# Two graph layers on one core: distances in row groups, messages by Strassen's product between the gate products

## The chip, the cores and the metric

The kernel runs on one core of a Trainium2 chip. A core has five engines that work side by side, each through its own queue in order: TensorE (PE in the profile) multiplies matrices, loading a stationary operand (PEld) and streaming a moving one past it into a memory of eight banks called PSUM; VectorE (DVE) and ScalarE (ACT) work elementwise and read PSUM; GpSimd (POOL) works elementwise on the main on-chip memory, SBUF, alone; SyncE (SP) issues transfers. The metric is the device time of one execution in microseconds. Before the change it was 2087.46 us, the median of three runs (2084.68 to 2087.62).

## What is computed

Two layers over 128 graphs of 128 nodes with 256 features, all in float32. The change lies in the second layer, which in the reference, cut to what matters, is this:

```python
xc = jnp.transpose(x, (0, 2, 1))
h = jax.nn.relu(_bn(_conv1d(xc, conv1_w, 0), bn1_g, bn1_b, bn1_m, bn1_v))
h = _bn(_conv1d(h, conv2_w, 8), bn2_g, bn2_b, bn2_m, bn2_v)
x_conv = jnp.transpose(jax.nn.relu(h + xc), (0, 2, 1))
s = x @ w_se.T + b_se                                   # 3 coordinates a node
sq = jnp.sum(s * s, axis=-1)
dist = sq[:, :, None] + sq[:, None, :] - 2.0 * jnp.einsum('bnd,bmd->bnm', s, s)
A = jnp.exp(-dist) * mask                               # mask: the adjacency
msg = jax.nn.relu(x @ w_msg.T + b_msg)
x_nmp = jnp.einsum('bnm,bmd->bnd', A, msg)
x_in = jnp.concatenate([x_conv, x_nmp], axis=-1)
gi = x_in @ w_ih.T + b_ih
gh = x @ w_hh.T + b_hh
# r, z: sigmoids of the first two thirds of gi + gh
nn_ = jnp.tanh(gi_n + r * gh_n)
return (1.0 - z) * nn_ + z * x                          # then x + this, layer norm
```

## The kernel before

There are three phases. The first (to about 740 us) runs layer 0 and the first convolution over pairs of graphs; it also makes the Fourier coefficients of the convolution's taps, with short products of 17 rows that lie in four row groups of TensorE's array (L408). The second (to about 930 us) multiplies in the Fourier domain (L503 to L530). The change is in the last phase, from 930 us to the end.

The last phase works on 32 groups of four graphs. For each group, PE runs these pieces:

- **gather** (`l1_gather`, L748): the product of messages and kernel matrix, 8 products in two banks, 16 passes in all. Every float32 product shows as two passes. ACT copies each bank to `nmpT`, and DVE makes the four sums `sm` from it.
- **messages** (`l1_project`, L693): 8 products of 128x128 by 128x256 into two banks; DVE adds the bias (L707), ACT applies the relu (L711). The function also starts the sums `sh` of x1T on POOL.
- **distances** (`l1_own`, L715, and `l1_kernel`, L735): each graph has 5 numbers a node, kept in 8 rows, in `left` and `right`. Sixteen graphs are turned together into 128 rows (`turned`). For each group, POOL multiplies `turned` by a mask for each graph into `own` (128x512), and one product of 128 rows by 512 columns gives the distances of four graphs in one bank. ACT takes the exponential (L743), DVE multiplies by the adjacency (L744) into `AT`.
- **gate** (`l1_gru`, L775), twice, each time for two graphs of a group in the two rows of a 2x2 block form: Strassen's product (Winograd's form) makes the gates with seven products instead of eight. Each of the seven has three parts (x1T, convolution, messages: `h`, `c`, `m`) of 384 columns in one bank, so six passes. DVE takes the banks in the order 0, 1, 5, 6, 4, 3, 2 (L797 to L805), POOL makes two sums beside it (L802, L803). Then comes a tail: tanh on ACT (L808), DVE L815 and L816, tanh (L817), DVE L819 to L822, and the layer norm (L247, L248, L152, L153, L255, L257).
- **synthesis** (`l1_synth`, L662), once for two groups: 16 products against a cosine table and 16 of 8 rows in four row groups, into four banks of the pool `acc`; DVE (L686) and ACT (L689) finish them, POOL makes the sums `sc`.

PSUM is split in two: `acc` has four banks for the synthesis, and `psC` has four which gather, messages, distances and gate take in turn. A piece that wants a bank waits until the one that used it four turns ago has been read.

PE's order is written out by hand, that of the other engines is a planner's: it simulates the program and gives each engine, whenever it is free, the ready operation that comes first in the program. The loop of the last phase (L843) is for each group g: start the loads of group g + 2; gather g; `own` and messages of g + 1; gate of the first half of g; distances of g + 1; in odd iterations the synthesis of the next two groups; gate of the second half of g. Ahead of the loop, a prologue makes own, messages, and distances of groups 0 and 1, the weight sums (`l1_factors`, L617) and the first synthesis.

Of the kernel before, what the change touches and what calls it, by code (L numbers as in the profile page):

```python
# [20 lines left out]
CO = 3  # L21
KD = 8
GD = P // KD
PAD = TAPS // 2
L = P + PAD
M = L
# [7 lines left out]
def gnn_layers_kernel(ctx: ExitStack, tc: tile.TileContext, a: dict, out: bass.AP):  # L34
# [332 lines left out]
    def l1_front(p):  # L367
        s = st[p]
        h = s["h"] = wk.tile([P, J, D], F32, tag="h", name=f"h_{p}")
        for j in range(J):  # L370
            ph = bank(f"conv1_ps_{p}_{j}")
            for c in range(NC):
                nc.tensor.matmul(  # L373
                    ph[:, 0 : D + CO], lhsT=s["x1T"][:, c, nodes(j)], rhs=conv1_w[:, c, :],
                    start=(c == 0), stop=(c == NC - 1),
                )
            nc.vector.tensor_tensor(h[:, j, :], ph[:, 0:D], shift1, ALU.add)
            nc.scalar.activation(coords[:, p * J + j, :], ph[:, D : D + CO], AF.Copy)
        nc.scalar.activation(h, h, AF.Relu)

    def l1_store(p):
# [173 lines left out]
    nc.vector.tensor_add(left[:, :, CO + 1], left[:, :, CO + 1], coords[:, :, 2])  # L555
    nc.vector.tensor_copy(right[:, :, CO], left[:, :, CO + 1])

    mask_i = cw.tile([P, GD], I32, tag="mask_i", name="mask_i")
    nc.gpsimd.iota(mask_i, pattern=[[-KD, GD]], base=0, channel_multiplier=1)
    mask_f = cw.tile([P, GD], F32, tag="mask_f", name="mask_f")  # L560
    nc.vector.tensor_copy(mask_f, mask_i)
    mask = cw.tile([P, GD], F32, tag="mask", name="mask")
    nc.vector.tensor_scalar(mask, mask_f, 0.0, None, ALU.is_ge)
    nc.vector.scalar_tensor_tensor(mask, mask_f, float(KD - 1), mask, ALU.is_le, ALU.mult)
    w_msg = weights("w_msgT", D)
    b_msg = rows("L1_gnn_b_msg", 0, D, cw)


# [36 lines left out]
    ci = cpool("ci", 3)  # L605
    cy = cpool("cy", 4)
    ck = cpool("ck", 2)
    acc = cpool("acc", 4, space=PSUM)
    psc = cpool("psC", 4, space=PSUM)

    def bankc(name):
        return psc.tile([P, 512], F32, tag="ps", name=name)

    cs = cpool("cs", 1)
    factors = {}

    def l1_factors():  # L617

        for kind, w in (("h", w_hh), ("c", w_ih[:, 0:NC]), ("m", w_ih[:, NC : 2 * NC])):
            t = cs.tile([P, 4, 3 * P], F32, tag=f"t{kind}", name=f"t_{kind}")  # L620
            b11, b12, b21, b22 = (w[:, c, h, :] for c in range(NC) for h in range(2))
            nc.vector.tensor_sub(t[:, 0, :], b12, b11)
            nc.vector.tensor_sub(t[:, 1, :], b22, t[:, 0, :])
            nc.vector.tensor_sub(t[:, 2, :], b22, b12)
            nc.vector.tensor_sub(t[:, 3, :], t[:, 1, :], b21)
            factors[kind] = (b11, b21, b22, t[:, 3, :], t[:, 0, :], t[:, 1, :], t[:, 2, :])

    def load_c(g):
        s = st[g] = {}
# [30 lines left out]


    def l1_synth(d):  # L662
        pcs = {}
        for e in range(2):
            s = st[2 * d + e]
            for c in range(NC):
                pc = pcs[e, c] = acc.tile([P, 512], F32, tag="acc", name=f"conv2_ps_{2 * d + e}_{c}")
                for q in range(G):
                    nc.tensor.matmul(  # L669
                        pc[:, nodes(q)], lhsT=sy[2 * d + e][0][:, q, c * P : (c + 1) * P], rhs=S,  # L670
                        start=(q == 0), stop=False, skip_group_check=True,
                    )
        for q in range(G):
            for e in range(2):
                for c in range(NC):
                    k = slice(32 * (NC * e + c), 32 * (NC * e + c) + ML)
                    nc.tensor.matmul(
                        pcs[e, c][:, nodes(q)], lhsT=sy[2 * d + e][1][k, q, :], rhs=SL[k, :],
                        start=False, stop=(q == G - 1), skip_group_check=True,
                    )  # L680
        for e in range(2):
            s = st[2 * d + e]
            s["xcT"] = ck.tile([P, NC, G * P], F32, tag="xcT", bufs=3, name=f"xcT_{2 * d + e}")
            for c in range(NC):
                dst = s["xcT"][:, c, :]
                nc.vector.scalar_tensor_tensor(  # L686
                    dst, pcs[e, c], scale2[:, c : c + 1], s["x1T"][:, c, :], ALU.mult, ALU.add
                )
                nc.scalar.activation(dst, dst, AF.Relu, bias=shift2[:, c : c + 1])  # L689
            l1_sums(2 * d + e, "c", s["xcT"], nc.gpsimd)  # L690


    def l1_project(g):  # L693
        s = st[g]
        x1T = s["x1T"]
        l1_sums(g, "h", x1T, nc.gpsimd)
        msg = ck.tile([P, G, D], F32, tag="msg", name=f"msg_{g}")
        for pr in range(G // 2):
            pm = bankc(f"msg_ps_{g}_{pr}")
            for j in range(2):  # L700
                q = 2 * pr + j
                for c in range(NC):
                    nc.tensor.matmul(  # L703
                        pm[:, j * D : (j + 1) * D], lhsT=x1T[:, c, nodes(q)], rhs=w_msg[:, c, :],
                        start=(c == 0), stop=(c == NC - 1),
                    )
            nc.vector.tensor_tensor(  # L707
                msg[:, 2 * pr : 2 * pr + 2, :], pm.rearrange("p (j e) -> p j e", j=2),
                b_msg.unsqueeze(1).to_broadcast([P, 2, D]), ALU.add,
            )  # L710
        nc.scalar.activation(msg, msg, AF.Relu)  # L711
        s["msg"] = msg


    def l1_own(g):  # L715
        if g % (GD // G) == 0:
            pt = bankc(f"turn_ps_{g}")
            for i, v in enumerate((left, right)):
                nc.tensor.transpose(
                    pt[:, nodes(i)], v[:, g * G : g * G + GD, :].rearrange("p q k -> p (q k)"), ident  # L720
                )
            turned = ck.tile([P, 2, P], F32, tag="turned", name=f"turned_{g}")
            nc.scalar.activation(turned.rearrange("p i n -> p (i n)"), pt[:, 0 : 2 * P], AF.Copy)
            st["turned"] = turned
        turned = st["turned"]

        own = ck.tile([P, G, P], F32, tag="own", name=f"own_{g}")
        lo = g * G % GD
        nc.gpsimd.tensor_tensor(
            own, turned[:, 1, :].unsqueeze(1).to_broadcast([P, G, P]),  # L730
            mask[:, lo : lo + G].unsqueeze(2).to_broadcast([P, G, P]), ALU.mult,
        )
        st[g].update(turned=turned, own=own)

    def l1_kernel(g):  # L735
        s = st[g]
        turned, own = s["turned"], s["own"]
        pd = bankc(f"dist_ps_{g}")
        nc.tensor.matmul(  # L739
            pd, lhsT=turned[:, 0, :], rhs=own.rearrange("p q n -> p (q n)"), start=True, stop=True  # L740
        )
        AT = ck.tile([P, G * P], F32, tag="AT", name=f"AT_{g}")
        nc.scalar.activation(AT, pd, AF.Exp, scale=-1.0)  # L743
        nc.vector.tensor_mul(AT, AT, s["adjT"].rearrange("p q n -> p (q n)"))  # L744
        s["AT"] = AT

# [15 lines left out]
    def l1_sums(g, kind, src, engine):  # L762

        v = src.rearrange("p c (r j n) -> p c r j n", r=G // 2, j=2)
        a11, a12, a21, a22 = (v[:, c, :, j, :] for j in range(2) for c in range(NC))
        t = ck.tile([P, 4, G // 2, P], F32, tag=f"s{kind}", name=f"s{kind}_{g}")
        s1, s2, s3, s4 = (t[:, i] for i in range(4))
        engine.tensor_tensor(s1, a21, a22, ALU.add)
        engine.tensor_tensor(s2, s1, a11, ALU.subtract)
        engine.tensor_tensor(s3, a11, a21, ALU.subtract)  # L770
        engine.tensor_tensor(s4, a12, s2, ALU.subtract)
        st[g][f"f{kind}"] = (a11, a12, s4, a22, s1, s2, s3)


    def l1_gru(g, pr):  # L775
        s = st[g]
        x1 = s["x1"]
        y = ck.tile([P, 2, D], F32, tag="y", name=f"y_{g}_{pr}")
        add, sub = ALU.add, ALU.subtract

        def product(i):
            pg = bankc(f"g_ps_{g}_{pr}_{i}")
            for k, (kind, lo) in enumerate((("h", 0), ("c", P), ("m", P))):
                nc.tensor.matmul(  # L784
# [45 lines left out]
    with tc.manual_schedule(engines={mybir.EngineType.PE}):  # L830
# [4 lines left out]
            load_x1(g)  # L835
            l1_own(g)
        for g in range(2):
            l1_project(g)
        for g in range(2):
            l1_kernel(g)  # L840
        l1_factors()
# [1 line left out]
        for g in range(NG):  # L843
            d = g // 2
            if g + 2 < NG:
                load_c(g + 2)
                if g % 2 == 0:
                    load_y(d + 1)
                load_x1(g + 2)
            l1_gather(g)  # L850
            if 2 <= g + 1 < NG:
                l1_own(g + 1)
                l1_project(g + 1)
            l1_gru(g, 0)
            if 2 <= g + 1 < NG:
                l1_kernel(g + 1)
            if g % 2 == 1 and d + 1 < ND:
                l1_synth(d + 1)
            l1_gru(g, 1)
# [42 lines left out]
```

## Time and profile before

| | us |
|---|---|
| median of three runs | 2087.46 |
| the profiled execution | 2086.79 |
| its span in the profile | 2085.0 |
| an even iteration of the last phase | 33.2 |
| an odd one, with a synthesis | 38.1 (every other one 38.3, with two transposes) |
| in an even one, DVE busy | 23.3 |
| TensorE on the chain of the whole span: gate products | 42% |
| messages | 5% |
| gather | 3% |
| distances | 1% |

The profile is one execution, recorded by the hardware. A line of a timeline has the start in us from the span's start, the length, the engine, the line of the kernel, the operation, the tiles written and read, and in brackets, where there are any, the idle time before it and what ended it. A line of the chain has start, length, engine and tile. The chain follows the work that ended last back to what released it: what isn't on it was hidden behind something else. PE's passes overlap at their ends (a pass of 384 columns shows as 0.486 us, though the next starts 0.322 us after it), so lengths of PE's work are taken from start to start. The granted clock of TensorE was 0.994 of full speed over the span.

### The profile page before, as it was taken

What the parts mean: (1) busy time and instruction counts of PE and PEld (TensorE: products, weight loads), DVE (VectorE), ACT (ScalarE), POOL (GpSimd) and SP (SyncE); (2) the same over time, 40 slices, a digit from 0 to 9 for tenths busy, and PEclk for the clock granted to TensorE, in tenths of its full rate; (3) what the DMA queues carried; (4) which work ended last, traced back from release to release, by engine and by line L of the source; (5) the groups of instructions that cost most, each with busy time, mean ns of one, the idle gap of its engine ahead of it and who ended that gap; (6) DMA issues with size and microseconds to landing.
All of it is one profiled execution on the core that took longest, in us unless ns stands there. A gap on an engine that the chain in (4) does not pass through costs nothing.

```text
span 2085.0 us, 27437 instructions
## 1 busy us (share of the span) xinstructions
PE 2043.7 (98%) x9025; PEld 1401.6 (67%) x9025; DVE 1433.0 (69%) x2856; ACT 744.0 (36%) x1484; POOL 672.9 (32%) x889
## 2 busy tenths in 40 slices
PE   8999999999999979999999999999999999999997
PEld 5666666766667658886666666666666666666664
DVE  7777777776777744447776766676767767766766
ACT  3555555555555511112222222222222222222221
POOL 1111111111111135553343444343434434443432
PEclk9999999999999999999999999999999999999999
DMA  3444444344444469993222122212212221221100
GB/s 117 137 145 138 137 147 144 133 144 137 140 145 133 153 228 318 305 302 119 62 82 68 54 74 72 69 60 72 78 51 75 70 73 56 67 72 56 36 25 21
DMA packets 191789, 235.39 MB, mean 113 GB/s; under 512 B 16400, under 2 KB 136736, under 8 KB 191648
## 3 DMA queue, kind: packets, MB, share of 16 engines
q1 hardware_dynamic: 186160, 229.44, 33.5%
q10 hardware_dynamic: 5488, 4.21, 0.7%
q8 instruction: 72, 1.18, 0.2%
q14 instruction: 69, 0.57, 0.1%
HBM read 129.77 MB, written 103.81 MB: 112 GB/s over the span
## 4 chain that ended last, share of the span: by engine, by line
PE 95%; DVE 2%; DMA 2%; ACT 1%; issue 1%; POOL 0%; POOLq 0%; ACTq 0%; DVEq 0%; SPq 0%
PE g_ps L784 42%; PE f_ps L303 10%; PE msg_ps L703 5%; PE gate_ps L308 5%; PE conv_ps L373 5%; PE y_ps L510 5%; PE mix_ps L329 3%; PE coef_ps L391 3%; PE nmp_ps L754 3%; PE conv_ps L669 3%; PE z_ps L523 2%; PE w_ps L408 2%; PE x1T_ps L270 2%; PE wl_ps L411 1%; PE xT_ps L270 1%; PE dist_ps L739 1%
## 5 line engine op out<-in xcount | busy, mean ns | idle before, releaser
L303 PE MATMUL f_ps<-w,xT 128*128 128x512 f32 x512 | 244.1, 600 | 0.1
L808 ACT ACTIVATE o<-o 128x1024 f32<-128x1024 f32 x64 | 67.6, 1057 | 335.6 <-DVE o L805 335.6
L152 POOL TENSOR_SCALAR rstd_b<-mv_b 128x2 f32<-128x2 f32 x64 | 12.2, 191 | 501.6 <-DVE mv_b L248 501.6
L152 POOL TENSOR_SCALAR rstd_a<-mv_a 128x2 f32<-128x2 f32 x64 | 12.2, 191 | 463.9 <-DVE mv_a L248 447.9
L784 PE MATMUL g_ps<-t_c,sc 128*128 128x384 f32 x384 | 155.2, 486 | 0.0
L784 PE MATMUL g_ps<-t_m,sm 128*128 128x384 f32 x384 | 155.2, 486 | 0.0
L784 PE MATMUL g_ps<-t_h,sh 128*128 128x384 f32 x384 | 155.2, 486 | 0.0
L257 ACT ACTIVATE y<-y,nb_b,rstd_b 128x256 f32<-128x256 f32 x128 | 69.9, 593 | 218.6 <-DVE nb_b L255 218.6
L308 PEld LDWEIGHTS gate_ps<-w,xT 128*128 128x128 f32 x512 | 98.2, 192 | 69.2 <-issue 61.8
L510 PE MATMUL y_ps<-wb,H 128*128 128x256 f32 x544 | 128.9, 380 | 4.7 <-DMA wb<-w_d 2.1
L308 PE MATMUL gate_ps<-w,xT 128*128 128x256 f32 x512 | 132.2, 381 | 0.0
L802 POOL TENSOR_TENSOR u<-u,p 128x512 f32<-128x512 f32 x64 | 81.1, 1267 | 155.4 <-DVE p L801 155.4
L303 PEld LDWEIGHTS f_ps<-w,xT 128*128 128x128 f32 x512 | 88.6, 192 | 62.6 <-issue 62.2
L312 ACT ACTIVATE hom<-f_ps,norm 128x256 f32<-128x256 f32 x128 | 60.5, 473 | 187.0 <-PE f_ps L303 187.0
L518 POOL TENSOR_TENSOR ws<-wb 128x512 f32<-128x512 f32 x67 | 94.8, 1416 | 88.7 <-PE z_ps L523 60.3
L373 PE MATMUL conv_ps<-conv_w,x1T 128*128 128x259 f32 x512 | 122.6, 381 | 0.0
L510 PEld LDWEIGHTS y_ps<-wb,H 128*128 128x128 f32 x544 | 102.8, 190 | 20.5 <-issue 5.1
L703 PE MATMUL msg_ps<-w_msgT_w,cx1T 128*128 128x256 f32 x512 | 115.6, 379 | 0.0
L784 PEld LDWEIGHTS g_ps<-t_m,sm 128*128 128x128 f32 x384 | 73.0, 190 | 50.9
L784 PEld LDWEIGHTS g_ps<-t_c,sc 128*128 128x128 f32 x384 | 73.0, 190 | 50.9
L784 PEld LDWEIGHTS g_ps<-t_h,sh 128*128 128x128 f32 x384 | 72.9, 190 | 50.9 <-issue 1.2
L373 PEld LDWEIGHTS conv_ps<-conv_w,x1T 128*128 128x128 f32 x512 | 97.2, 190 | 14.4
(219 smaller groups left out, 4622.4 us busy)
## 6 DMA issues: line engine op xcount, KB each, us to landing
wb<-w_d SPq DMA_DIRECT2D x68, 512.0 KB
w_d<-w_o SPq DMA_DIRECT2D x256, 128.0 KB
y_d<-yb SPq DMA_DIRECT2D x68, 256.0 KB
x<-in_x SPq DMA_DIRECT2D x64, 256.0 KB
x_d<-x SPq DMA_DIRECT2D x64, 256.0 KB
x1T_d<-x1T SPq DMA_DIRECT2D x64, 256.0 KB
cx1T<-x1T_d SPq DMA_DIRECT2D x64, 256.0 KB
yt<-y_d SPq DMA_DIRECT2D x32, 512.0 KB
```

What stands on the lines that cost most here:

```text
L257: nc.scalar.activation(dst[:, q, :], src[:, q, :], AF.Identity, bias=nb[:, q : q + 1], scale=rstd[:, q : q + 1],)
L270: nc.tensor.transpose(t[:, (c * J + j) * P : (c * J + j + 1) * P], src[:, j, c * P : (c + 1) * P], ident,)
L303: nc.tensor.matmul(pf, lhsT=xT[:, c, nodes(j)], rhs=w0[:, c, 0 : 2 * D], start=(c == 0), stop=(c == NC - 1),)
L308: nc.tensor.matmul(pg[:, j * D : (j + 1) * D], lhsT=xT[:, c, nodes(j)], rhs=w0[:, c, 2 * D : 3 * D], start=(c == 0), stop=(c == NC - 1),)
L329: nc.tensor.matmul(pm[:, j * D : (j + 1) * D], lhsT=adjT_[:, j, :], rhs=hom[:, j, :], start=True, stop=True,)
L373: nc.tensor.matmul(ph[:, 0 : D + CO], lhsT=s["x1T"][:, c, nodes(j)], rhs=conv1_w[:, c, :], start=(c == 0), stop=(c == NC - 1),)
L510: nc.tensor.matmul(py[:, blk, :], lhsT=coefs(blk if k == 0 else 2 * k + 1 - blk, c), rhs=w[:, c, blk, :], start=(c == 0), stop=(c == NC - 1),)
L518: nc.gpsimd.tensor_tensor(ws, w[:, :, 0, :], w[:, :, 1, :], ALU.add)
L703: nc.tensor.matmul(pm[:, j * D : (j + 1) * D], lhsT=x1T[:, c, nodes(q)], rhs=w_msg[:, c, :], start=(c == 0), stop=(c == NC - 1),)
L784: nc.tensor.matmul(pg[:, lo : lo + 3 * P], lhsT=s[f"f{kind}"][i][:, pr, :], rhs=factors[kind][i], start=(k == 0), stop=(k == 2), skip_grou ...
L802: nc.gpsimd.tensor_tensor(u4, u2, p5, add)
L808: nc.scalar.activation(rz, rz, AF.Tanh, scale=0.5)
```

## The change

In the distances, the coordinates are stored in another order, so that in `turned` the graphs with the same place q in their groups share 32 rows. `own` becomes one 128x128 product with a mask of one column a group, and the distances of a group are four products of 32 rows by 128 columns, each in its own row group and its own bank. The four banks are one tile of the pool `acc`, which now has one tile of four banks that distances and synthesis take in turn. They are computed ahead of the first gate half instead of behind it, and `own` and the sums `sh` are made one group earlier, with three buffers for `sh` and one for `sm`.

The messages of groups 2 to 31 use Strassen's product as the gate does: seven products of two 128x128 halves. They come in four portions (products 0 and 1; 5 and 6; 4 and 3; 2), one bank each, issued in the first gate half ahead of its third, fourth, fifth and sixth product. DVE adds the portions up in seven operations of 128x256, POOL in two. Groups 0 and 1 keep the old form under the name `l1_project_first`.

```diff
-            nc.scalar.activation(coords[:, p * J + j, :], ph[:, D : D + CO], AF.Copy)
+            b = p * J + j
+            slot = b // GD * GD + b % G * GR + b % GD // G
+            nc.scalar.activation(coords[:, slot, :], ph[:, D : D + CO], AF.Copy)
...
+    def right_factors(pool, name, b11, b12, b21, b22):
+
+        t = pool.tile([P, 4, b11.shape[-1]], F32, tag=f"t{name}", name=f"t_{name}")
+        nc.vector.tensor_sub(t[:, 0, :], b12, b11)
+        nc.vector.tensor_sub(t[:, 1, :], b22, t[:, 0, :])
+        nc.vector.tensor_sub(t[:, 2, :], b22, b12)
+        nc.vector.tensor_sub(t[:, 3, :], t[:, 1, :], b21)
+        return b11, b21, b22, t[:, 3, :], t[:, 0, :], t[:, 1, :], t[:, 2, :]
...
-    acc = cpool("acc", 4, space=PSUM)
+    acc = cpool("acc", 1, space=PSUM)
     psc = cpool("psC", 4, space=PSUM)
...
+    nc.vector.tensor_sub(b_rest, b_msg[:, P:D], b_msg[:, 0:P])
...
     def l1_synth(d):
+        four = acc.tile([P, 4, 512], F32, tag="acc", name=f"conv2_ps_{d}")
...
     def l1_project(g):
...
+        def products(*which):
+            pm = bankc(f"msg_ps_{g}_{which[0]}")
+            for k, i in enumerate(which):
+                for r in range(2):
+                    nc.tensor.matmul(
+                        pm[:, (2 * k + r) * P : (2 * k + r + 1) * P],
+                        lhsT=s["fh"][i][:, r, :], rhs=m_factors[i], start=True, stop=True,
+                    )
...
+        pa, pb = products(0, 1)
+        v.tensor_tensor(u1, pa, bias_m[0], add)
+        v.tensor_tensor(o[:, :, 0, 0, :], pb, u1, add)
+        yield
+        pa, pb = products(5, 6)
+        v.tensor_tensor(u2, pa, u1, add)
+        v.tensor_tensor(u3, pb, u2, add)
+        yield
+        pa, pb = products(4, 3)
+        v.tensor_tensor(p5, pa, bias_m[1], add)
+        v.tensor_tensor(o[:, :, 1, 0, :], u3, pb, sub)
+        nc.gpsimd.tensor_tensor(u4, u2, p5, add)
+        nc.gpsimd.tensor_tensor(o[:, :, 1, 1, :], u3, p5, add)
+        yield
+        (pa,) = products(2)
+        v.tensor_tensor(o[:, :, 0, 1, :], pa, u4, add)
+        nc.scalar.activation(msg, msg, AF.Relu)
+        yield
...
     def l1_own(g):
...
-        own = ck.tile([P, G, P], F32, tag="own", name=f"own_{g}")
-        lo = g * G % GD
-        nc.gpsimd.tensor_tensor(
-            own, turned[:, 1, :].unsqueeze(1).to_broadcast([P, G, P]),
-            mask[:, lo : lo + G].unsqueeze(2).to_broadcast([P, G, P]), ALU.mult,
+        own = ck.tile([P, P], F32, tag="own", name=f"own_{g}")
+        nc.gpsimd.tensor_scalar(
+            own, turned[:, 1, :], mask[:, g % GR : g % GR + 1], None, ALU.mult
         )
...
     def l1_kernel(g):
...
-        pd = bankc(f"dist_ps_{g}")
-        nc.tensor.matmul(
-            pd, lhsT=turned[:, 0, :], rhs=own.rearrange("p q n -> p (q n)"), start=True, stop=True
-        )
+        pd = acc.tile([P, G, 512], F32, tag="acc", name=f"dist_ps_{g}")
+        for q in range(G):
+            k = slice(q * P // G, (q + 1) * P // G)
+            nc.tensor.matmul(
+                pd[:, q, 0:P], lhsT=turned[k, 0, :], rhs=own[k, :], start=True, stop=True
+            )
...
     def l1_sums(g, kind, src, engine):
-        t = ck.tile([P, 4, G // 2, P], F32, tag=f"s{kind}", name=f"s{kind}_{g}")
+        t = ck.tile([P, 4, G // 2, P], F32, tag=f"s{kind}", bufs={"h": 3, "c": 2, "m": 1}[kind], name=f"s{kind}_{g}")
...
-    def l1_gru(g, pr):
+    def l1_gru(g, pr, between=()):
...
         def product(i):
+            if next(made) > 1:
+                next(between, None)
...
                 load_x1(g + 2)
+                l1_own(g + 2)
+                l1_sums(g + 2, "h", st[g + 2]["x1T"], nc.gpsimd)
             l1_gather(g)
             if 2 <= g + 1 < NG:
-                l1_own(g + 1)
-                l1_project(g + 1)
-            l1_gru(g, 0)
-            if 2 <= g + 1 < NG:
                 l1_kernel(g + 1)
+            l1_gru(g, 0, l1_project(g + 1) if 2 <= g + 1 < NG else ())
             if g % 2 == 1 and d + 1 < ND:
                 l1_synth(d + 1)
             l1_gru(g, 1)
```

More of the change, by code (lines that the diff above doesn't have):

```diff
@@ L23 @@
 GD = P // KD
+GR = GD // G
 PAD = TAPS // 2
@@ L556, in gnn_layers_kernel @@
     nc.vector.tensor_copy(right[:, :, CO], left[:, :, CO + 1])
[L558 to L564, printed above, removed]
-    w_msg = weights("w_msgT", D)
+    row_i = cw.tile([P, G, GR], I32, tag="row_i", name="row_i")
+    nc.gpsimd.iota(row_i, pattern=[[-GR * KD, G], [-KD, GR]], base=0, channel_multiplier=1)
+    row_f = cw.tile([P, G, GR], F32, tag="row_f", name="row_f")
+    nc.vector.tensor_copy(row_f, row_i)
+    hit = cw.tile([P, G, GR], F32, tag="hit", name="hit")
+    nc.vector.tensor_scalar(hit, row_f, 0.0, None, ALU.is_ge)
+    nc.vector.scalar_tensor_tensor(hit, row_f, float(KD - 1), hit, ALU.is_le, ALU.mult)
+    mask = cw.tile([P, GR], F32, tag="mask", name="mask")
+    nc.vector.tensor_add(mask, hit[:, 0, :], hit[:, 1, :])
+    for q in range(2, G):
+        nc.vector.tensor_add(mask, mask, hit[:, q, :])
+    w_msg = weights("w_msgT", D)
+    def right_factors(pool, name, b11, b12, b21, b22):
[5 more added lines that the diff above has]
+        return b11, b21, b22, t[:, 3, :], t[:, 0, :], t[:, 1, :], t[:, 2, :]
+    m_factors = right_factors(
+        cw, "msg", *(w_msg[:, c, h * P : (h + 1) * P] for c in range(NC) for h in range(2))
+    )
     b_msg = rows("L1_gnn_b_msg", 0, D, cw)
@@ L614, in gnn_layers_kernel @@
     cs = cpool("cs", 1)
+    b_rest = ones
+    nc.vector.tensor_sub(b_rest, b_msg[:, P:D], b_msg[:, 0:P])
     factors = {}
@@ L619, in l1_factors @@
         for kind, w in (("h", w_hh), ("c", w_ih[:, 0:NC]), ("m", w_ih[:, NC : 2 * NC])):
[L620 to L626, printed above, removed]
+            factors[kind] = right_factors(cs, kind, *(w[:, c, h, :] for c in range(NC) for h in range(2)))
     def load_c(g):
@@ L666, in l1_synth @@
             for c in range(NC):
-                pc = pcs[e, c] = acc.tile([P, 512], F32, tag="acc", name=f"conv2_ps_{2 * d + e}_{c}")
+                pc = pcs[e, c] = four[:, NC * e + c, :]
                 for q in range(G):
@@ L694, in l1_project, with sums, l1_project_first @@
         s = st[g]
-        x1T = s["x1T"]
-        l1_sums(g, "h", x1T, nc.gpsimd)
-        msg = ck.tile([P, G, D], F32, tag="msg", name=f"msg_{g}")
+        msg = s["msg"] = ck.tile([P, G, D], F32, tag="msg", name=f"msg_{g}")
+        o = msg.rearrange("p (r j) (h n) -> p r j h n", r=2, h=2)
+        v, add, sub = nc.vector, ALU.add, ALU.subtract
+        def products(*which):
[6 more added lines that the diff above has]
+                    )
+            return [pm[:, 2 * k * P : 2 * (k + 1) * P].rearrange("p (r n) -> p r n", r=2) for k in range(len(which))]
+        def sums(name):
+            return ck.tile([P, 2, P], F32, tag=f"m{name}", bufs=1, name=f"m{name}_{g}")
+        u1, u2, u3, u4, p5 = (sums(q) for q in ("u1", "u2", "u3", "u4", "p5"))
+        bias_m = [q.unsqueeze(1).to_broadcast([P, 2, P]) for q in (b_msg[:, 0:P], b_rest)]
+        pa, pb = products(0, 1)
[16 more added lines that the diff above has]
+        yield
+    def l1_project_first(g):
+        s = st[g]
+        msg = s["msg"] = ck.tile([P, G, D], F32, tag="msg", name=f"msg_{g}")
         for pr in range(G // 2):
@@ L700, in l1_project @@
             for j in range(2):
-                q = 2 * pr + j
                 for c in range(NC):
                     nc.tensor.matmul(
-                        pm[:, j * D : (j + 1) * D], lhsT=x1T[:, c, nodes(q)], rhs=w_msg[:, c, :],
-                        start=(c == 0), stop=(c == NC - 1),
+                        pm[:, j * D : (j + 1) * D], lhsT=s["x1T"][:, c, nodes(2 * pr + j)],
+                        rhs=w_msg[:, c, :], start=(c == 0), stop=(c == NC - 1),
                     )
@@ L711, in l1_project @@
         nc.scalar.activation(msg, msg, AF.Relu)
-        s["msg"] = msg
     def l1_own(g):
@@ L737, in l1_kernel @@
         turned, own = s["turned"], s["own"]
-        pd = bankc(f"dist_ps_{g}")
-        nc.tensor.matmul(
-            pd, lhsT=turned[:, 0, :], rhs=own.rearrange("p q n -> p (q n)"), start=True, stop=True
-        )
-        AT = ck.tile([P, G * P], F32, tag="AT", name=f"AT_{g}")
-        nc.scalar.activation(AT, pd, AF.Exp, scale=-1.0)
+        pd = acc.tile([P, G, 512], F32, tag="acc", name=f"dist_ps_{g}")
[3 more added lines that the diff above has]
+                pd[:, q, 0:P], lhsT=turned[k, 0, :], rhs=own[k, :], start=True, stop=True
+            )
+        AT = ck.tile([P, G * P], F32, tag="AT", name=f"AT_{g}")
+        nc.scalar.activation(
+            AT.rearrange("p (q n) -> p q n", q=G), pd[:, :, 0:P], AF.Exp, scale=-1.0
+        )
         nc.vector.tensor_mul(AT, AT, s["adjT"].rearrange("p q n -> p (q n)"))
@@ L772, in l1_sums @@
         st[g][f"f{kind}"] = (a11, a12, s4, a22, s1, s2, s3)
-    def l1_gru(g, pr):
+    def l1_gru(g, pr, between=()):
         s = st[g]
+        between = iter(between)
         x1 = s["x1"]
@@ L779, in l1_gru @@
         add, sub = ALU.add, ALU.subtract
+        made = iter(range(7))
         def product(i):
+            if next(made) > 1:
+                next(between, None)
             pg = bankc(f"g_ps_{g}_{pr}_{i}")
@@ L837, in gnn_layers_kernel @@
         for g in range(2):
-            l1_project(g)
+            l1_sums(g, "h", st[g]["x1T"], nc.gpsimd)
+            l1_project_first(g)
         for g in range(2):
```

## The prediction

> **What bounds the kernel now.** I read the page's busy times and its chain of waits first, then the chain in order of time inside the last phase, then the timelines of VectorE (DVE) and GpSimd (POOL) beside it.
>
> ```profile
> PE 2043.7 (98%) x9025; PEld 1401.6 (67%) x9025; DVE 1433.0 (69%) x2856; ACT 744.0 (36%) x1484; POOL 672.9 (32%) x889
> PE 95%; DVE 2%; DMA 2%; ACT 1%; issue 1%; POOL 0%; POOLq 0%; ACTq 0%; DVEq 0%; SPq 0%
> ```
>
> TensorE is the end-to-end bound. In the last phase nothing else is on the chain, and each piece starts where the last one stopped:
>
> ```profile
> 1543.34 1.78 PE nmp_ps L754 x16
> 1545.12 3.46 PE msg_ps L703 x16
> 1548.58 13.54 PE g_ps L784 x42
> 1562.13 0.86 PE dist_ps L739 x2
> 1562.98 3.57 PE conv_ps L669 x32
> 1566.56 1.10 PE conv_ps L677 x32
> 1567.66 13.74 PE g_ps L784 x42
> ```
>
> So a microsecond of TensorE work removed here is gained, unless a wait takes its place. An iteration of the group loop takes 33.2 us (even) or 38.1 us (odd, with the synthesis). DVE is busy 23.3 us of 33.2 and 25.8 of 38.0 there. It isn't the bound on average, but it works in bursts. One gate product is 6 passes in 1.93 us (13.54/7).
>
> **Part 1, messages.** Removed: 16 passes of 256 columns, 3.46 us. Added: 7 products x 2 halves x 2 passes = 28 passes of 128 columns. The nearest row is nmp_ps: 16 such passes in 1.78, 0.111 each, so 3.12 us; by L669 (3.57/32) it is the same, and with that line's entry of 0.1 counted once for each of four portions it would be 3.5. I take 3.12: **-0.34** an iteration (bounds -0.34 to +0.06). Groups 0 and 1 keep the old form, so 30 iterations (1 to 30): -10.2 us.
>
> **Part 2, distances.** Removed: 0.86. Added: 4 products x 2 passes, 32 rows by 128 columns, in four row groups and four banks. The tap products of the first phase have just that shape with 512 columns:
>
> ```profile
> 312.43 1.07 PE w_ps L408 x8
> 313.50 0.98 PE wl_ps L411 x2
> 314.47 0.59 PE x1T_ps L270 x4
> 315.06 1.72 PE f_ps L303 x4
> ```
>
> A 512-column pass is 0.43 (1.72/4), so eight in a row would be 3.44, and they took 1.07: two passes deep (0.86) and 0.21 on top. For 128 columns that gives 2 x 0.111 + 0.21 = 0.43, and about 0.1 on the way back to full products (wl_ps takes 0.98 for two passes of 0.43; the first gate products behind L677 also lose 0.1). By L677, 1.10/32 x 8 = 0.28 and 0.2 for both switches, 0.48. I take 0.50: **-0.36**, 30 times -10.8, and -0.7 for the two in the prologue. Bounds: 0.28, and 1.09 if nothing overlapped (8 x 0.111 + 0.2).
>
> The Trainium skill (TensorEngine Tiling (Array Packing), Key Properties and Theoretical Speedup) promises up to 4x for 32 rows, but says that a change of tiling mode drains the array. By the 4x alone the distances would cost 0.22 and the 30 iterations would gain 19; the rows above show 3.2x and 0.2 to 0.3 us of switching, and the rows are used.
>
> **Part 3, work that moves to DVE and POOL.** DVE's two message adds (0.68) become seven of 128x256 out of PSUM. The first phase has that shape (h<-conv_ps at L377: 0.42), so +1.6 us an iteration, DVE from 70 to 75%. POOL gets two 128x256 adds (0.73, as L768) and its `own` shrinks from 1.04-1.16 to something between 0.19 (the smallest tensor_scalar) and that. I cost these at nothing, because behind the third product DVE idles 1.2 us before each of the next three (L801, L804, L805); without that cover it is 1.6 us each, 47 in all. The new right factors and `b_rest` are five small DVE operations (at most 0.55 each, the 384-wide ones of L622) in the phase before, where DVE waits 1.9 us of every 2.6.
>
> **Part 4, lost cover.** The 3.46 us of messages between gather and gate gave ACT and DVE time for nmpT and its sums. Product 5 needs s2 8.3 us after the gather began (T0) instead of 10.4; s2 now ends at T0+7.3, and 0.5 later is still in time. Group 31, which has no messages before its gate, runs its 84 gate passes in 27.11 us without a gap. Nothing lost.
>
> **Part 5, the new wait.** Messages and gate products share four PSUM banks in rotation. Until now product 0's bank came round again at product 4, T0+13. Now the order is nmp, nmp, 0, 1, portion 1, 5, portion 2, 6, and portion 2 takes product 0's bank: with 1.78 + 0.50 + 2 x 1.93 + 0.89 + 1.93 it wants it at **T0+8.97**, and product 6 wants product 1's at T0+9.86. They are free when DVE has done u1 (L797) and o (L798). An even iteration (T0 = 1509.99):
>
> ```profile
> 1513.66 1.21 DVE L816 SCALAR_TENSOR_TENSOR o<-o 128x512 f32<-128x512 f32 x1
> 1514.80 0.95 DVE L768 TENSOR_TENSOR sm<-nmpT 128x256 f32<-128x256 f32 x1
> 1515.67 0.68 DVE L707 TENSOR_TENSOR msg<-msg_ps,L_gnn_b_msg_b 128x512 f32<-128x512 f32 x1
> 1518.74 0.68 DVE L707 TENSOR_TENSOR msg<-msg_ps,L_gnn_b_msg_b 128x512 f32<-128x512 f32 x1
> 1519.34 0.67 DVE L822 TENSOR_TENSOR y<-o,cx 128x512 f32<-128x512 f32 x1
> 1519.94 0.68 DVE L797 TENSOR_TENSOR u<-g_ps,bias 128x512 f32<-128x512 f32 x1
> ```
> ```profile
> 1513.41 0.91 POOL L769 TENSOR_TENSOR sc<-sc,xcT 128x256 f32<-128x256 f32 x1
> 1514.29 1.17 POOL L771 TENSOR_TENSOR sh<-cx1T,sh 128x256 f32<-128x256 f32 x1
> 1515.42 0.91 POOL L771 TENSOR_TENSOR sc<-xcT,sc 128x256 f32<-128x256 f32 x1
> ```
>
> DVE alternates: one step of the last half's tail (L815 to L822), then one ready operation that comes earliest in the program. After the change the adjacency product (L744, 0.68) is ready there, as the distances moved ahead; it takes the first message slot (1515.67), and u1 the second (1518.74). L798 follows L822. In odd iterations these slots lie at T0+4.57 and T0+7.64: u1 ends at 8.32, o at 9.52, no wait. In even ones u1 would run from 8.75 to 9.43. But POOL is at its sums until T0+6.34, and DVE operations with both inputs in SBUF lengthen beside them (L816 1.21 instead of 0.68, L768 0.95 instead of 0.41), each ending 0.3 to 0.55 after a POOL operation ends. The message add, fed from PSUM, wasn't lengthened. L744 has two SBUF inputs, and takes that slot: I add 0.53, as L816 shows. Then u1 ends at 9.96 (TensorE waits 0.99), portion 2 at 10.85, o at 11.16 (0.31 more), and 0.05 for restarting: **+1.35** in 15 even iterations, +20.2 us. Bounds: 0, if DVE comes to u1 a slot and a step (1.2) sooner, and 2.6, if as much later. What queues behind is everything on TensorE; DVE itself catches up before portion 3.
>
> No run here shows L744 beside POOL: its longest is 0.687. The Trainium skill (SBUF — State Buffer, Who interferes with whom) says that a DVE instruction with two SBUF inputs contends with a GpSimd instruction that reads SBUF, one with a single SBUF input not; by it the 0.53 stands, while by L744's own row u1 would end at 9.43, the wait be 0.8, and the total 8 us lower.
>
> **Part 6, prologue.** The one four-bank tile makes distances 0, the exponential, distances 1, the exponential and the synthesis wait for each other: 0.58 (L743) and some 0.3 of handing over, twice, less if hidden. The synthesis, started at 938.10, would start between 939.2 and 941.1 (the latter if both exponentials stay behind ACT's relu at 938.02 to 939.08); DVE reads its result 0.9 after it is ready. So +0.2 to +2.1; I take +1.
>
> **Sum:** -10.2 - 10.8 - 0.7 + 1 + 20.2 = -0.5. Against the profiled execution's 2086.79 (span 2085.0 and 1.8 around it) 2086.3; the median of the runs is 0.67 above that execution: **2087**. About 0.2% (4.2 us) is what this kernel's timing can tell from no change.
>
> **Rivals.** (a) *The wait hardly comes*: L744 is not lengthened, or u1 comes a slot earlier. For it: odd iterations show 0.65 us of slack in the same order. Against: POOL's eight sums stand at the start of every even iteration. Without lengthening 2079, without any wait 2067. (b) *DVE's backlog decides in odd iterations too*: u1 and o come one slot and step later (1.2 us), because an added operation or the two-stage sums stand ahead of them. From u1's end at 8.97 on, each further 0.1 costs 1.5 us over fifteen iterations. Even ones then wait 2.55, odd ones 0.55 + 0.25: 15 x (3.35 - 1.35) = +30, 2117; half of it 2102. For it: slack in odd iterations is only 0.34 at L798. Against: all the new DVE work is later in the program than u1. (c) *The row groups don't overlap*: 1.09 instead of 0.50, 30 x 0.59 = +18, 2105; w_ps speaks against it.
>
> **How the numbers follow.** Forecast 0.34 (own range 2081 to 2093: of it 0.24 within 4.2 us, 0.06 below, 0.04 above); (a) 0.36, of it 0.33 below; (b) 0.25, (c) 0.05, all above. Faster 0.39, same 0.27, slower 0.34. The range reaches into (a) and (b) as far as 2069 and 2104.
>
> **What would show it.** Messages: 28 passes in about 3.1 us an iteration, in four portions. Distances: 0.5. TensorE idle of 1 us before portion 2 and 0.3 before product 6 in even iterations, ended by DVE L797 and L798, none in odd ones. L744 at about 1.2 in even iterations and 0.68 in odd. The prediction is wrong if even iterations show no gap, if odd ones do, or if a portion's passes take over 0.12.

## The result, and the profile after

| | before | after |
|---|---|---|
| median of seven runs, us | 2086.28 (2082.94 to 2087.62) | 2095.73 (2092.88 to 2103.11) |
| ratio | | 1.0051, 95% interval 1.0035 to 1.0066 |
| the profiled execution | 2086.79 | 2103.11 |
| its span | 2085.0 | 2101.3 |
| last phase: first turn to the gather of group 0 (prologue) | 13.67 | 20.48 |
| gather of group 0 to gather of group 31 (loop) | 1099.70 | 1101.66 |
| an odd iteration, mean | 38.16 | 37.62 |
| an even one, mean | 33.19 | 33.89 |
| from the gather of group 31 to the end | 42.43 | 42.42 |

The change made the kernel 9.45 us slower by the medians, not equal. The profiled execution of after is 7.4 above its own median, and the excess lies before the changed code: the first turn of the last phase starts at 936.74 us here, at 929.20 in the profile before, and at 924.9 to 928.4 in the seven experiments that are built from after, whose first two phases are the same as its. So the last phase is compared by itself, as in the lower half of the table: prologue +6.8, loop +2.0, together +8.8. That accounts for the medians to within 0.7 us. All comparisons of pieces below are of this kind.

The page of after, busy times and the shares of the chain:

```profile
PE 2042.7 (97%) x9577; PEld 1408.6 (67%) x9577; DVE 1471.0 (70%) x3014; ACT 745.4 (35%) x1484; POOL 722.4 (34%) x949
PE 79%; DVE 9%; POOL 4%; DMA 3%; issue 2%; ACT 2%; SPq 0%; ACTq 0%; POOLq 0%; DVEq 0%
```

TensorE was 95% of the chain before and is 79% now; DVE went from 2% to 9%. DVE's total load hardly rose (1433 to 1471 us). The chain has moved to it because TensorE now stops for it. TensorE's waits in the last phase say where (us in total, times, longest):

```profile
PE msg_ps L721 <- DVE u L860: 10.8, 14, 0.8
PE dist_ps L794 <- POOL own L783: 2.8, 1, 2.8
PE dist_ps L794 <- ACT AT L798: 0.8, 1, 0.8
PE conv_ps L685 <- ACT AT L798: 0.7, 1, 0.7
```

The same view of before has 0.2 us behind the first turn. The first line is the predicted wait: portion 2 of the messages waits for u1 (L797 of before is L860 now) once in each even iteration but the first, which makes no messages, and the last. The other three happen once each, in the prologue, and weren't foreseen in this size.

**An even iteration.** TensorE, from the gather of an even iteration (T0 = 1525.05; start, length, line, tiles):

```profile
1525.05 1.95 PE L811 MATMUL nmp_ps<-AT,msg 128*128 128x128 f32 x16
1526.92 0.50 PE L794 MATMUL dist_ps<-own,turned 32*128 32x128 f32 x8
1527.36 0.91 PE L847 MATMUL g_ps<-w_hhT_w,cx1T 128*128 128x384 f32 x2
1528.11 0.81 PE L847 MATMUL g_ps<-w_ihT_w,xcT 128*128 128x384 f32 x2
...
1535.16 1.16 PE L721 MATMUL msg_ps<-t_msg,sh 128*128 128x128 f32 x8 [0.84 <-DVE u L860]
1536.36 0.91 PE L847 MATMUL g_ps<-t_h,sh 128*128 128x384 f32 x2
```

VectorE and GpSimd in the same stretch:

```profile
1528.72 1.21 DVE L879 SCALAR_TENSOR_TENSOR o<-o 128x512 f32<-128x512 f32 x1
1529.86 0.94 DVE L825 TENSOR_TENSOR sm<-nmpT 128x256 f32<-128x256 f32 x1
1530.73 1.21 DVE L801 TENSOR_TENSOR AT<-AT,cadjT 128x512 f32<-128x512 f32 x1
...
1534.43 0.68 DVE L860 TENSOR_TENSOR u<-g_ps,bias 128x512 f32<-128x512 f32 x1
1535.03 0.67 DVE L885 TENSOR_TENSOR y<-o,cx 128x512 f32<-128x512 f32 x1
1535.63 0.68 DVE L861 TENSOR_TENSOR o<-g_ps,u 128x512 f32<-128x512 f32 x1
```
```profile
1529.35 1.17 POOL L828 TENSOR_TENSOR sh<-cx1T,sh 128x256 f32<-128x256 f32 x1
1530.48 0.91 POOL L828 TENSOR_TENSOR sc<-xcT,sc 128x256 f32<-128x256 f32 x1
1531.37 1.56 POOL L783 TENSOR_SCALAR own<-turned,mask 128x128 f32<-128x128 f32 x1
```

Read the three columns of starts against each other. POOL's last two sums run until 1531.4, and each DVE operation beside them with two SBUF inputs is stretched: the adjacency product (L744 of before, L801 now) takes 1.21 us in these iterations and 0.68 in the odd ones. So u1 starts at T0 + 9.38, and portion 2 starts 0.05 after it ends. It had its operands long before.

**The prologue.** TensorE, and the end of POOL's queue:

```profile
937.01 7.07 PE L759 MATMUL msg_ps<-w_msgT_w,cx1T 128*128 128x256 f32 x32
946.88 0.50 PE L794 MATMUL dist_ps<-own,turned 32*128 32x128 f32 x8 [2.80 <-POOL own L783]
948.20 0.50 PE L794 MATMUL dist_ps<-own,turned 32*128 32x128 f32 x8 [0.81 <-ACT AT L798]
949.41 6.78 PE L685 MATMUL conv_ps<-S,yt 128*128 128x128 f32 x32 [0.71 <-ACT AT L798]
...
957.22 2.05 PE L811 MATMUL nmp_ps<-AT,msg 128*128 128x128 f32 x16
```
```profile
944.56 0.92 POOL L828 TENSOR_TENSOR sh<-cx1T,sh 128x256 f32<-128x256 f32 x1
945.47 2.96 POOL L783 TENSOR_SCALAR own<-turned,mask 128x128 f32<-128x128 f32 x3
```

The same in before:

```profile
929.48 7.07 PE L703 MATMUL msg_ps<-w_msgT_w,cx1T 128*128 128x256 f32 x32
936.39 1.88 PE L739 MATMUL dist_ps<-own,turned 128*128 128x512 f32 x4
938.10 3.73 PE L669 MATMUL conv_ps<-S,yt 128*128 128x128 f32 x32
...
942.87 2.05 PE L754 MATMUL nmp_ps<-AT,msg 128*128 128x128 f32 x16
```
```profile
933.79 2.70 POOL L729 TENSOR_TENSOR own<-turned,mask 128x512 f32<-128x512 f32 x2
```

From the messages' start to the gather it was 13.39 us before (929.48 to 942.87) and is 20.21 now. Three pieces make the 6.8: the distances start 9.87 us after the messages instead of 6.91 (+2.96); from there to the synthesis it is 2.53 instead of 1.71 (+0.82); from the synthesis to the gather 7.81 instead of 4.77 (+3.04). The last is no wait at all: the same 32 passes took 6.78 us where they took 3.73 before. The windows say why (stretch, its length, busy us with the number of instructions of PE, PEld, DVE, ACT, POOL, then the granted clock, the DMA share and GB/s):

```profile
948.00:949.00 1.00, 0.50 (x8) 0.34 (x8) 0.91 (x2) 0.29 (x2) 0.54 (x2) 0.89 1.01 344
950.00:951.00 1.00, 1.00 (x6) 1.00 (x6) 0.88 (x2) 0.00 (x0) 0.10 (x1) 0.50 1.04 349
956.00:957.00 1.00, 1.00 (x30) 0.88 (x32) 0.00 (x0) 0.00 (x0) 0.00 (x0) 1.00 1.04 363
```

After the three waits the granted clock of TensorE is 0.50 from 948.78 to 955.61. The synthesis lies in 6.20 us of that, busy throughout, and half of 6.20 is 3.10: the clock accounts for the whole loss.

### The profile page after: what moved, and what is told of

Its sections match the earlier page's. It is cut to its first block, busy times and chain, and to the rows that moved or that the text cites. A ratio compares the mean times of both kernels' runs of the same rounds, so it can differ in the third digit from the quotient of the medians.

```text
span 2101.3 us, 28808 instructions
## 1 busy us (share of the span) xinstructions
PE 2042.7 (97%) x9577; PEld 1408.6 (67%) x9577; DVE 1471.0 (70%) x3014; ACT 745.4 (35%) x1484; POOL 722.4 (34%) x949
## 4 chain that ended last, share of the span: by engine, by line
PE 79%; DVE 9%; POOL 4%; DMA 3%; issue 2%; ACT 2%; SPq 0%; ACTq 0%; POOLq 0%; DVEq 0%
PE g_ps L847 31%; PE f_ps L304 10%; PE y_ps L513 5%; PE conv_ps L374 5%; PE gate_ps L309 5%; PE msg_ps L721 4%; PE mix_ps L330 3%; PE coef_ps L394 3%; PE z_ps L526 2%; PE w_ps L411 2%; PE x1T_ps L271 2%; PE nmp_ps L811 2%; PE wl_ps L414 2%; PE conv_ps L685 2%; DMA x_d<-x 1%
## 5 line engine op out<-in xcount | busy, mean ns | idle before, releaser
L513 PEld LDWEIGHTS y_ps<-wb,H 128*128 128x128 f32 x544 | 103.9, 192 | 20.2 <-issue 4.2
L847 PE MATMUL g_ps<-w_hhT_w,cx1T 128*128 128x384 f32 x256 | 108.2, 504 | 0.0
L847 PE MATMUL g_ps<-w_ihT_w,xcT 128*128 128x384 f32 x256 | 103.5, 486 | 0.0
L847 PE MATMUL g_ps<-w_ihT_w,nmpT 128*128 128x384 f32 x256 | 103.5, 486 | 0.0
```

The costliest lines, as they stand in the source:

```text
L513: nc.tensor.matmul(py[:, blk, :], lhsT=coefs(blk if k == 0 else 2 * k + 1 - blk, c), rhs=w[:, c, blk, :], start=(c == 0), stop=(c == NC - 1),)
L847: nc.tensor.matmul(pg[:, lo : lo + 3 * P], lhsT=s[f"f{kind}"][i][:, pr, :], rhs=factors[kind][i], start=(k == 0), stop=(k == 2), skip_grou ...
```

## The experiments

Every kernel but the seventh, which is built from before, has the same prologue and loop as after except for the edit shown. Kernels 1 to 4 were timed beside one set of runs of before (median 2084.35), 5 to 8 beside another (2085.60). Parts of the last phase of each, in us:

| kernel | prologue | odd | even | loop | median | ratio (95%) |
|---|---|---|---|---|---|---|
| before | 13.67 | 38.16 | 33.19 | 1099.70 | 2086.28 | |
| after | 20.48 | 37.62 | 33.89 | 1101.66 | 2095.73 | 1.0051 (1.0035 to 1.0066) |
| 1: `own` of groups 0 and 1 on ScalarE | 18.11 | 37.62 | 33.89 | 1101.56 | 2091.12 | 1.0034 (1.0022 to 1.0047) |
| 2: and distances between the messages | 14.00 | 37.62 | 33.88 | 1101.47 | 2087.49 | 1.0014 (1.0005 to 1.0023) |
| 3: three buffers for `sc` | 19.91 | 37.61 | 32.63 | 1082.65 | 2076.44 | 0.9963 (0.9949 to 0.9976) |
| 4: portions in the second gate half | 19.74 | 38.62 | 32.75 | 1099.61 | 2091.38 | 1.0037 (1.0025 to 1.0050) |
| 5: distances as a fifth portion | 20.39 | 37.60 | 33.40 | 1094.08 | 2085.41 | 1.0000 (0.9991 to 1.0008) |
| 6: messages in the old form | 20.13 | 37.93 | 32.96 | 1092.43 | 2084.81 | 0.9994 (0.9985 to 1.0003) |
| 7: buffers of 3 in the kernel before | 13.67 | 38.16 | 33.19 | 1099.70 | 2085.45 | 1.0002 (0.9993 to 1.0011) |
| 8: edits of 2 and 3 together | 14.00 | 37.62 | 32.63 | 1082.79 | 2068.22 | 0.9917 (0.9904 to 0.9931) |

### 1. The prologue's `own` on another engine

```diff
-        nc.gpsimd.tensor_scalar(
-            own, turned[:, 1, :], mask[:, g % GR : g % GR + 1], None, ALU.mult
-        )
+        if g < 2:
+            nc.scalar.activation(own, turned[:, 1, :], AF.Copy, scale=mask[:, g % GR : g % GR + 1])
+        else:
+            nc.gpsimd.tensor_scalar(
+                own, turned[:, 1, :], mask[:, g % GR : g % GR + 1], None, ALU.mult
+            )
```

> Theory: the prologue costs about 8 us because own of groups 0 and 1 stands on POOL behind the twelve sums of three groups (2.8 us of wait before the first distances), and the waits together let TensorE's granted clock fall to 0.5 for the synthesis (3.2 us). With own of groups 0 and 1 on ACT the first distances follow the messages with under 0.3 us of wait, the clock stays at 1, and the time from the first message pass to the first gather falls from 20.2 us to 13.5 to 15. Time 2089 (from 2095.7). Rival: the serial chain distances, exponential, distances, exponential through the one four-bank tile is what costs; then only the 2.8 us are gained, the clock still falls, 2093. Even iterations unchanged at 33.9 to 34.0 us under both.

Measured: 2091.12. The prologue fell by 2.4 us only. TensorE of this kernel:

```profile
935.64 0.50 PE L797 MATMUL dist_ps<-own,turned 32*128 32x128 f32 x8
938.76 0.50 PE L797 MATMUL dist_ps<-own,turned 32*128 32x128 f32 x8 [2.61 <-ACT AT L801]
939.98 5.47 PE L685 MATMUL conv_ps<-S,yt 128*128 128x128 f32 x32 [0.72 <-ACT AT L801]
```

The wait for `own` is gone, and a wait of nearly the same length has come one piece later. Now the exponential of group 0, which has to empty the one tile of four banks, stands on ScalarE behind the relu of the messages of group 1 (here the queue of ScalarE, in order):

```profile
937.16 1.06 ACT L767 ACTIVATE msg<-msg 128x1024 f32<-128x1024 f32 x1 [3.08 <-DVE msg L763]
938.13 0.58 ACT L801 ACTIVATE AT<-dist_ps 128x512 f32<-128x512 f32 x1
```

So both causes hold, POOL's queue and the single tile, and the time lies between the two expectations. By the trace the rival came closer: it had 2.8 us gained and the clock still falling, and the prologue gained 2.4. The synthesis again took far longer than 3.73.

### 2. And the distances between the messages of groups 0 and 1

```diff
-        for g in range(2):
-            l1_sums(g, "h", st[g]["x1T"], nc.gpsimd)
-            l1_project_first(g)
-        for g in range(2):
-            l1_kernel(g)
+        for g in range(2):
+            l1_sums(g, "h", st[g]["x1T"], nc.gpsimd)
+        for g in range(2):
+            l1_project_first(g)
+            l1_kernel(g)
```

This stands on top of edit 1.

> As the run before, and in the prologue the distances of group 0 are issued between the messages of groups 0 and 1. Theory: the wait before the second distances (0.8) goes too, the one before the synthesis (0.7) stays; 12.7 to 14 us from the first message pass to the first gather, time 2088. Rival: DVE's message adds and weight sums are what the synthesis' results wait for, so nothing is gained over the run before.

Measured: 2087.49. TensorE:

```profile
931.53 0.50 PE L797 MATMUL dist_ps<-own,turned 32*128 32x128 f32 x8
931.96 3.72 PE L759 MATMUL msg_ps<-w_msgT_w,cx1T 128*128 128x256 f32 x16
935.61 0.50 PE L797 MATMUL dist_ps<-own,turned 32*128 32x128 f32 x8
936.84 3.84 PE L685 MATMUL conv_ps<-S,yt 128*128 128x128 f32 x32 [0.72 <-ACT AT L801]
```

The messages of group 1 now cover the exponential of group 0. One wait of 0.72 is left, and the synthesis is back at 3.84. The prologue costs 14.00, 0.3 more than before. With the three waits (4.3 us) the synthesis lost 3.0 us, with two (3.3 us) 1.7, with one of 0.72 nearly nothing. So the slow clock is a consequence of the waits; in after it added 3.0 us to the 3.8 that they cost themselves. In kernel 1 the clock was at 0.50 for 3.41 us instead of 6.83, and half of 3.41 is again the loss of 1.7.

### 3. Three buffers for the sums of the convolution

```diff
-        nmpT = ck.tile([P, NC, G * P], F32, tag="nmpT", name=f"nmpT_{g}")
+        nmpT = ck.tile([P, NC, G * P], F32, tag="nmpT", bufs=1, name=f"nmpT_{g}")
...
-        t = ck.tile([P, 4, G // 2, P], F32, tag=f"s{kind}", bufs={"h": 3, "c": 2, "m": 1}[kind], name=f"s{kind}_{g}")
+        t = ck.tile([P, 4, G // 2, P], F32, tag=f"s{kind}", bufs={"h": 3, "c": 3, "m": 1}[kind], name=f"s{kind}_{g}")
```

With two buffers, the sums `sc` of the second of the two groups that one synthesis makes must wait until the gate of the group before has read its own; that puts them at the start of every even iteration. With three they run in the odd iteration. `nmpT` goes from two buffers to one to make room.

> Three buffers for the sums sc (and one for nmpT to make room), so that POOL makes all eight sc sums in the odd iteration and only four sh sums stand at the start of an even one. Theory: the wait of portion 2 in even iterations comes from DVE operations with two SBUF inputs being held up beside POOL; L801 falls from 1.13 to about 0.7 there, u1 ends at T0+8.3 as in odd iterations, the idle of 0.84 and 0.3 us goes, even iterations take 32.6 instead of 34.0: -20 us, 2075. Rival: the adjacency product and DVE's backlog alone hold u1 back; even iterations stay at 33.6 or more, 2090 or more.

Measured: 2076.44, even iterations 32.63, no wait left in the loop. The same stretch of VectorE, T0 = 1506.44:

```profile
1509.93 0.77 DVE L879 SCALAR_TENSOR_TENSOR o<-o 128x512 f32<-128x512 f32 x1
1510.63 0.41 DVE L825 TENSOR_TENSOR sm<-nmpT 128x256 f32<-128x256 f32 x1
1510.96 0.68 DVE L801 TENSOR_TENSOR AT<-AT,cadjT 128x512 f32<-128x512 f32 x1
...
1514.04 0.68 DVE L860 TENSOR_TENSOR u<-g_ps,bias 128x512 f32<-128x512 f32 x1
```

The operations come in the same order as in after, with 0.77, 0.41 and 0.68 us in place of 1.21, 0.94 and 1.21. u1 starts at T0 + 7.60 instead of 9.38, in time. Nothing was taken from VectorE: only POOL's work was moved away from beside it. That shows the cause of the wait.

### 4. The portions in the second gate half

```diff
-            l1_gru(g, 0, l1_project(g + 1) if 2 <= g + 1 < NG else ())
+            l1_gru(g, 0)
...
-            l1_gru(g, 1)
+            l1_gru(g, 1, l1_project(g + 1) if 2 <= g + 1 < NG else ())
```

> The four message portions go into the second gate half instead of the first. Theory: the wait belongs to the head of the first half, where the sums sm, the adjacency product and the tail stand ahead of u1; in the second half these are absent, so even iterations take 32.6 and odd ones 37.6, about 2075. Rival: seven message adds are too much for DVE in any half, and in odd iterations the synthesis' four results stand ahead of u1 in the second half; odd iterations get a wait of 0.6 us or more each, even ones lose theirs, 2083 or more.

Measured: 2091.38. The even iterations lose the wait but for 0.1 us (32.75 against 32.63 in kernel 3), and the odd ones get it, 15 times (the waits, then the chain in an odd iteration):

```profile
PE msg_ps L721 <- DVE u L860: 11.3, 15, 0.8
```
```profile
1502.76 1.40 DVE xcT L702 x2
1504.16 0.61 DVE u L860
1504.77 0.04 issue
1504.81 1.16 PE msg_ps L721 x8
```

In odd iterations the second half begins behind the synthesis, whose four results (L702) stand ahead of u1 on VectorE. The rival was right: the place for the portions matters as much as POOL's load, since each half has something ahead of u1.

### 5. The distances as a fifth portion

```diff
+    def both(g):
+        yield from l1_project(g)
+        l1_kernel(g)
+        yield
...
-                l1_kernel(g + 1)
-            l1_gru(g, 0, l1_project(g + 1) if 2 <= g + 1 < NG else ())
+            l1_gru(g, 0, both(g + 1) if 2 <= g + 1 < NG else ())
```

This takes the adjacency product out of the place ahead of u1.

> The distances of the next group are issued as a fifth portion, before the last product of the first gate half, so that the adjacency product L801 no longer stands ahead of u1. Theory: u1 starts one slot and step earlier (about 1.2 us, and L801 was itself lengthened by 0.45), the wait of portion 2 in even iterations goes, though POOL's eight sums are still there: even iterations 32.6, odd 37.6, prologue unchanged, 2076. Rival: the lengthened sums s3, L816, s1 alone keep u1 behind T0+8.9; a wait of 0.3 or more stays, 2082 or more.

Measured: 2085.41, half of the gain that was expected. The wait for u1 is shorter, not gone:

```profile
PE msg_ps L721 <- DVE u L860: 1.6, 8, 0.4
```

Three things were overlooked. With the distances gone from behind the gather, portion 2 is also due 0.63 us earlier, by what they cost there (see below). And POOL's sums still stand beside the other operations ahead of u1: in the iteration with the longest wait u1 ended at T0 + 9.04, only 1.0 us earlier than in after, and portion 2 started 0.05 later. Third, most of what is left is lost behind portion 2, where product 6 waits for o (L861). In the last even iteration, which doesn't wait, portions 2 and 3 start at T0 + 8.49 and 11.31; in the others portion 2 starts at 8.68 to 9.09 and portion 3 at 11.96 to 12.37. Even iterations took 33.4 to 33.8, the last one 32.6.

### 6. The messages in the old form, the distances in the new

```diff
+                l1_project_first(g + 1)
                 l1_kernel(g + 1)
-            l1_gru(g, 0, l1_project(g + 1) if 2 <= g + 1 < NG else ())
+            l1_gru(g, 0)
```

> The distance part alone: messages in the old form (sixteen passes of 256 columns, two DVE adds) between gather and distances, all else as after the change. Theory: no portion takes a gate product's bank early, so no wait in the loop; each of 30 iterations gains what the distances save (0.86 less 0.43 and 0.1 of switching: 0.33), 10 us, and the prologue still loses 7: 2082 to 2084. Rival: moving the adjacency product to the head of the first half delays DVE enough by itself; even iterations above 33.2 and the time 2091 or more.

Measured: 2084.81, no wait in the loop. This prices the two savings apart. The distances alone save 0.23 us an iteration (38.16 to 37.93, 33.19 to 32.96); the messages, by the step from here to kernel 3, another 0.33 (32.96 to 32.63). The chain of this kernel:

```profile
1510.80 1.78 PE nmp_ps L811 x16
1512.59 3.46 PE msg_ps L759 x16
1516.04 0.43 PE dist_ps L794 x8
```

### 7. The same buffers in the kernel before

```diff
-        t = ck.tile([P, 4, G // 2, P], F32, tag=f"s{kind}", name=f"s{kind}_{g}")
+        t = ck.tile([P, 4, G // 2, P], F32, tag=f"s{kind}", bufs={"h": 2, "c": 3, "m": 1}[kind], name=f"s{kind}_{g}")
```

> The kernel before with three buffers for sc and one for sm, nothing else. Theory: three buffers gain only because they remove a wait that the change made, so here, where TensorE never waits in the loop, 0 (ratio 1.000). Rival: POOL's contention costs time of its own; then 5 us or more faster here too.

Measured: 2085.45 against 2085.60, the loop equal to 0.01 us. The buffers are worth nothing where there is no wait: the 19 us of kernel 3 belong to the wait that the change brought, and aren't a gain that the kernel before had left lying.

### 8. Both repairs

> Three buffers for sc, one for nmpT, own of groups 0 and 1 on ACT and the distances of group 0 between the messages of groups 0 and 1. Theory: the two losses are independent, so their gains add: 2095.7 - 19.3 - 8.2 = 2068, 16 below the kernel before; nothing on TensorE waits in the loop and the gather of group 0 begins 14.5 us after the turn, as before. Rival: the prologue's gain depended on the waits of the loop (both read the same sums on POOL); then no better than 2076.

Measured: 2068.22, 17.4 us and 0.83% (0.69 to 0.96%) below before. The two losses are independent: prologue as in kernel 2, loop as in kernel 3. Of the unforeseen waits of TensorE one is left:

```profile
PE conv_ps L685 <- ACT AT L801: 0.7, 1, 0.7
```

## Why the prediction was wrong, step by step

The forecast was no change; the kernel became slower by 9.45 us. The loop was predicted at -0.8 us (30 x -0.70 and +20.2) and measured at +2.0. The prologue was predicted at +0.3 (+1 and -0.7) and measured at +6.8. Two thirds of the error are the prologue.

**The step that failed is Part 6**, "So +0.2 to +2.1; I take +1". It priced the hand-overs of the one tile of four banks. It asked when the exponentials release that tile, not when the distances can begin. The diff moves the sums `sh` one group ahead, so that in the prologue twelve of them, of three groups, are ready at once; `own` of groups 0 and 1 stands behind all twelve on POOL (945.47), where it stood behind eight before. The text looked at that queue only for the loop, where it costs nothing. That was +2.96, and behind it the hand-overs added only +0.82. And the waits together brought the clock down, +3.04 in this execution, which Part 6 had no term for.

The tile alone was sized too low as well. In kernel 1, where `own` is out of the way, the synthesis starts 11.34 us after the messages (939.98 - 928.64) instead of 8.62: +2.72, above the bound of 2.1. Part 6 had seen this case, both exponentials behind ScalarE's relu and the synthesis 3.0 later. But it took off 0.9 because VectorE reads the synthesis' result later, while on TensorE the gather follows right behind the synthesis (in before at 942.87) and is put off with it. Without POOL's queue and without that chain, in kernel 2, the prologue is 14.00.

**Part 5, the new wait, was right** in its place, cause and size, in even iterations alone. u1 ends at T0 + 10.06 (forecast 9.96), and the adjacency product is lengthened by 0.53 (1.21 against 0.68), as forecast. Between after and kernel 3 the start of portion 2 differs by 1.00 (T0 + 10.11 against 9.11; forecast 0.99) and that of product 6 by 1.31 (T0 + 11.31 against 10.00; forecast 1.35). That the sizes agree so closely is partly luck: u1 ends 0.10 later than put down, but portion 2 is also due 0.14 later (9.11 against 8.97), and the two nearly cancel. Taking the wait away gave 19.0 us in the loop; 20.2 had been put down, as the last even iteration has no sums `sh` of a later group to make and doesn't wait. The Trainium skill (SBUF — State Buffer, Who interferes with whom) states that a DVE instruction with two SBUF inputs contends with a GpSimd instruction that reads SBUF, and one with at most one SBUF input (outside certain modes) doesn't. No run had shown it for this operation. Now there is one, and it agrees: with two SBUF inputs the adjacency product takes 1.21 us beside POOL's sums and 0.68 without, while u1, fed from PSUM and one SBUF tile, keeps to 0.672 to 0.692 in all its 64 executions, 16 of them beside POOL.

**Part 1, messages: right.** -0.34 put down, -0.33 measured.

**Part 2, distances: right in kind, off in size.** The row groups overlap: eight passes show as 0.43 on the chain. But what the array lost at the changes was put too low. The gather's last piece runs 0.09 longer before the distances (1525.05 to 1526.92 is 1.87, not 1.78), and the first gate pair behind them takes 0.75 (1527.36 to 1528.11) where a pair takes 0.645. The cost is 0.43 + 0.09 + 0.10 = 0.63, not 0.50, so the saving is 0.23 and not 0.36: 30 x 0.13 = 3.9 us less. Together with 0.3 for the messages, -1.2 for the wait and -0.47 in iteration 0, which makes neither messages nor distances, that is 2.5 of the 2.8 us by which the loop missed. The trace shows where the -0.47 lies: in before TensorE stops once in that iteration until ScalarE has copied `nmpT` (third gate pair at 946.41, 1.00 us after the second instead of 0.645, and the next 0.1 late), and in after it doesn't. Why ScalarE is in time there was not tested.

**Parts 3 and 4, what was costed at nothing: right in the loop.** With POOL's sums moved away no wait is left there (kernel 3), so the seven additions on VectorE and the lost cover cost nothing. One bound was wrong: `own`, put between 0.19 and 1.16 us, takes 1.37 (median, 0.60 to 1.56). In the loop it is hidden; in the prologue it is on the path.

**The rivals.** (a) fell: the adjacency product is lengthened. (b) fell: no odd iteration waits, and they are 0.54 shorter; kernel 4 shows that an odd iteration would wait if the portions stood behind the synthesis. (c) fell: 0.43, not 1.09. The time was above the forecast for none of their reasons.

## What to carry to other kernels

When work is issued a step earlier, price the prologue as its own small kernel: there everything becomes ready at once, and what the first product needs can stand last in some queue. A stage whose saving is a few tenths per iteration is easily outweighed by one wait that a shared resource brings; here moving four sums on another engine out of the stretch, by a third buffer, was worth more (19.0 us) than the change's own 16.5 (30 x 0.55). And where an early wait is removed, expect the next one: look at which engine and buffer ends it, then remove both.

## What the runs showed of the hardware

- The granted clock fell to half although no idle time was longer than 2.8 us: 2.80, 0.81 and 0.71, with pieces of some 0.4 us between them. It stayed at 0.50 for 6.83 us, and 32 passes took 6.78 us instead of 3.73. Waits of 2.61 and 0.72 had it too (3.41 us at 0.50, 5.47 for the passes), a single 0.72 not (3.84). The Trainium skill (TensorE: Matmul & The Clock Gate, Part 1) states that the clock halves after at least one idle window of about 3.4 us. Here the array was never idle for so long at a stretch: in the 3.41 us ahead of the fall it was busy for 1.01 us in after and 0.66 in kernel 1. The measurement decides: nearly idle was enough.
- The price of such waits isn't fixed. Kernels 3 to 6 have the prologue of after and the same 6.83 us at 0.50, but the fall came at another moment: 4.28, 3.36, 5.37 and 4.82 us of it lay in the synthesis instead of 6.20, and the time from the synthesis to the gather was longer than before by 2.1, 1.7, 2.7 and 2.4 us instead of 3.0, half each time.
- A POOL multiplication of 128x128 by one column of factors took 1.37 us (median; 0.60 to 1.56), longer than the 128x512 product of two tensors that it replaced (1.16; 1.04 to 1.49). A quarter of the elements did not make it shorter here; why was not tested.
- Changing between full products and four row groups cost 0.09 us in and 0.10 us out here, 0.19 us on a piece of 0.43.
